# Row gathers for an attention ranking model: one tile moved to SyncE, single-SBUF-input VectorE operations, c inside the contraction, and a reordered last block

## The chip, the cores and the metric

The kernel runs on one core of a Trainium2 chip. The metric is device time in microseconds; the kernel before took 15,447.25 us (median of three runs, 15,437.24 to 15,494.0). Besides the timed runs there is one profiled execution, which took 11,178.86 us.

## The reference

For each of 16,384 users there are 69 item ids and one label id, all rows of a table `emb` of 100,001 rows with 96 floats. What is computed, cut to what matters:

```python
u = emb[batch_user]                       # 16384 x 69 x 96
ql = emb[batch_label[:, 0]]               # 16384 x 96
q = jnp.broadcast_to(ql[:, None, :], u.shape)
z = jnp.concatenate([q, u, q - u, q * u], axis=-1)
h = _dice(z @ W1 + b1, a1, EPS_DICE)      # 64 wide; dice(x) = (a*(1-p)+p)*x, p = sigmoid(x*s)
att = (h @ W2 + b2) @ W3 + b3             # one weight per item
pre = jnp.where((batch_user < ITEM_NUM)[..., None], u * att, 0.0)
pooled = jnp.einsum('gf,bfe->bge', window, pre)       # 69 items into 10 groups
x = jnp.concatenate([pooled.reshape(B, 10 * 96), ql], axis=-1)
h = _dice(_bn_eval(x @ Wf1 + bf1), af1)   # 200 wide
h = _dice(_bn_eval(h @ Wf2 + bf2), af2)   # 80 wide
return h @ Wf3 + bf3
```

An id of 100,000 counts as no item. The first layer is rewritten in both kernels as u (W1[1] - W1[2]) + (q*u) W1[3] + c, with c = q (W1[0] + W1[2]) + b1, one value per user and hidden unit.

## The kernel before

The users go in 32 blocks of 512. A block has 69 chunks of 512 (user, item) pairs, four tiles of 128 rows each: 64 main chunks (8 users by 64 items) and 5 tail chunks (one item of all 512 users). Two chunks make a pair; there are 1104 pairs, and the work of one pair is spread over several steps of a hand-made schedule.

Ids at or above 100,000 are mapped to an extra row of zeros (`rows`), by a VectorE operation with the ids as both inputs:

```python
nc.vector.scalar_tensor_tensor(rows, ids[:, 0:NT], float(ITEM_NUM), ids[:, 0:NT], ALU.is_ge, ALU.add)   # L110
```

GpSimd gathers each tile of 128 rows (L229); TensorE turns it; VectorE multiplies by q and ScalarE copies out of PSUM:

```python
def fetch(i):
    ...
    for t in range(4):
        gather(u[:, 4 * j + t, :], rows[n][:, 4 * k + t : 4 * k + t + 1])                   # L229
        nc.tensor.transpose(ptr[:, t * P : (t + 1) * P], u[:, 4 * j + t, :], ident)         # L325
    ... nc.vector.tensor_tensor(quT[:, j, :] ..., ptr ..., by_field(q ...), ALU.mult)       # L328
    nc.scalar.copy(uT[:, j, :], ptr)                                                        # L336
```

The label rows of blocks 1 to 31 are fetched by SyncE, one transfer per row, after 32 ids have been loaded from HBM into its registers:

```python
def head_gather(n, part):
    ...
    _, at = nc.values_load_multi_w_load_instructions(lab[n : n + 1, part * NLD : (part + 1) * NLD], ...)   # L252
    for i, row in enumerate(at):
        nc.sync.dma_start(out=qs[n][p + i : p + i + 1, k, :], in_=emb[bass.ds(row, 1), :])                 # L260
```

c is put into the accumulator before the matmuls: a matmul of zeros opens the bank, ScalarE writes c over it, and the first layer adds to it:

```python
def seed(i):
    nc.tensor.matmul(ph, zrow[:, 0:P], zrow, start=True, stop=False)                       # L295
    nc.scalar.copy(ph.rearrange(...), by_field(cs[n0][0][:, k0 * NS : (k0 + 1) * NS]))     # L298
def hidden(i, ph, uT, quT):
    for w, x, last in [(A, uT, False), (Wp, quT, True)]:
        for j in range(2):
            nc.tensor.matmul(ph[j * H1 : (j + 1) * H1, :], w, x[:, j, :], start=False, stop=last)   # L343
    nc.scalar.activation(y, ph, AF.Sigmoid, scale=S_DICE)                                  # L345
    nc.scalar.activation(y, y, AF.Identity, bias=a1c, scale=na1c)                          # L346
    nc.vector.tensor_mul(y, ph, y)                                                         # L347
```

Four pairs' attention weights are turned together and spread over the groups, then used as the moving side of the pooling:

```python
    nc.vector.tensor_scalar(w, pt[:, :, :, 0:2] ..., bb, None, ALU.add)                    # L373
    nc.vector.tensor_tensor(rw ..., R ..., w ..., ALU.mult)                                # L376, both in SBUF
    nc.tensor.matmul(pa[...], u[:, 4 * j + t, :], rw[:, i % 4, j, t, :], ...)              # L393
    nc.vector.tensor_copy(pooled[n][...], pa ...)                                          # L402
```

The three last layers of a block (L423, L437, L446) run in ten steps beside the next block; each dice ends in a product of two SBUF tiles (`nc.vector.tensor_mul(x1, x1, g1)`, L430, and L441). The result of a block goes out by SyncE (L449). [The set-up, with some twenty small loads, is left out here.]

Of the kernel before, what the change touches and what calls it, by code (L numbers as in the profile page):

```python
# [30 lines left out]
BF16 = mybir.dt.bfloat16  # L32
# [5 lines left out]
P = 128  # L38
# [16 lines left out]
NLD = 32  # L55
# [6 lines left out]


@with_exitstack
def rec_kernel(
# [3 lines left out]
    lab: bass.AP,  # L69
    emb: bass.AP,  # L70
    W1: bass.AP,
    b1: bass.AP,
    a1: bass.AP,
    W2T: bass.AP,
    b2: bass.AP,
    W3: bass.AP,
    b3: bass.AP,
    Wf1: bass.AP,
    bf1: bass.AP,
    af1: bass.AP,  # L80
    Wf2: bass.AP,
    bf2: bass.AP,
    af2: bass.AP,
    Wf3: bass.AP,
    bf3: bass.AP,
    wrow: bass.AP,
    wtile: bass.AP,
# [7 lines left out]
    tpool = ctx.enter_context(tc.tile_pool(name="tpool", bufs=5))  # L95
    hpool = ctx.enter_context(tc.tile_pool(name="hpool", bufs=3))
    ypool = ctx.enter_context(tc.tile_pool(name="ypool", bufs=8))
# [3 lines left out]

    def load_ids(n):
        ids = ipool.tile([P, NCOL], I32, tag="ids", name=f"ids{n}")
        nc.sync.dma_start(out=ids, in_=idx[n : n + 1].rearrange("o p n -> (o p) n"))
        return ids

    def map_ids(n, ids):

        rows = ipool.tile([P, NT], I32, tag="rows", name=f"rows{n}")
        nc.vector.scalar_tensor_tensor(rows, ids[:, 0:NT], float(ITEM_NUM), ids[:, 0:NT], ALU.is_ge, ALU.add)  # L110
        return rows

    ids, rows = {0: load_ids(0)}, {}
    rows[0] = map_ids(0, ids[0])
# [5 lines left out]
    w1 = const.tile([E, 4, H1], F32, name="w1")  # L120
    nc.sync.dma_start(out=w1, in_=W1.rearrange("(k e) h -> e k h", e=E))
    Cq = const.tile([E + 1, 2, H1], F32, name="Cq")
    for i in range(2):
        nc.vector.tensor_add(Cq[0:E, i, :], w1[:, 0, :], w1[:, 2, :])
    nc.sync.dma_start(
        out=Cq[E : E + 1], in_=b1.rearrange("(o q h) -> o q h", o=1, q=1).to_broadcast([1, 2, H1])
    )
    Wp = w1[:, 3, :]
    A = const.tile([E, H1], F32, name="A")
    nc.vector.tensor_sub(A, w1[:, 1, :], w1[:, 2, :])  # L130

    qTs = []
    for i in range(2):
        t = const.tile([E + 1, BLK + NS], F32, name=f"qT{i}")
        nc.vector.memset(t[:, BLK:], 0.0)
        nc.vector.memset(t[E : E + 1, :], 1.0)
        qTs.append(t)

    def column(ap, name, n, copies=1):
        t = const.tile([n * copies, 1], F32, name=name)  # L140
        for i in range(copies):
            nc.sync.dma_start(out=t[i * n : (i + 1) * n, :], in_=ap.rearrange("(n o) -> n o", o=1))
        return t

    def one_minus(t, name):
        r = const.tile(list(t.shape), F32, name=name)
        nc.vector.tensor_scalar(r, t, -1.0, 1.0, ALU.mult, ALU.add)
        return r

    a1c = column(a1, "a1c", H1, 2)  # L150
    na1c = one_minus(a1c, "na1c")


    w2t = const.tile([H2, 2, H1], F32, name="w2t")
    for i in range(2):
        nc.sync.dma_start(out=w2t[:, i, :], in_=W2T)
    w3 = const.tile([H2, 1], F32, name="w3")
    nc.sync.dma_start(out=w3, in_=W3)
    w3b = const.tile([H2, E], F32, name="w3b")
    nc.vector.tensor_copy(w3b, w3.to_broadcast([H2, E]))  # L160
    b2c = column(b2, "b2c", H2)
    b2m = const.tile([H2, P], F32, name="b2m")
    nc.vector.tensor_copy(b2m, b2c.to_broadcast([H2, P]))
    b3r = const.tile([P, 1], F32, name="b3r")
    nc.sync.dma_start(out=b3r, in_=b3.rearrange("(o n) -> o n", o=1).to_broadcast([P, 1]))
# [6 lines left out]
    R = const.tile([P, 2 * G], F32, name="R")  # L172
    nc.scalar.dma_start(out=R, in_=wtile)
    wr = const.tile([E, NTAIL, G], F32, name="wr")
    nc.scalar.dma_start(out=wr, in_=wrow.rearrange("(o f) g -> o f g", o=1).to_broadcast([E, NTAIL, G]))


    wf1 = const.tile([E, G + 1, D1], F32, name="wf1")
    nc.scalar.dma_start(out=wf1, in_=Wf1.rearrange("(k e) n -> e k n", e=E))
    wf2 = const.tile([DH, 2, D2], F32, name="wf2")  # L180
    nc.scalar.dma_start(out=wf2, in_=Wf2.rearrange("(k e) n -> e k n", e=DH))
    wf3 = const.tile([D2, 1], F32, name="wf3")
    nc.scalar.dma_start(out=wf3, in_=Wf3)
    bf1c = [column(bf1[i * DH : (i + 1) * DH], f"bf1c{i}", DH) for i in range(2)]
    af1c = [column(af1[i * DH : (i + 1) * DH], f"af1c{i}", DH) for i in range(2)]
    bf2c = column(bf2, "bf2c", D2)
    af2c = column(af2, "af2c", D2)
    bf3c = column(bf3, "bf3c", 1)
    naf1c = [one_minus(t, f"naf1c{i}") for i, t in enumerate(af1c)]
    naf2c = one_minus(af2c, "naf2c")  # L190
    sbf1 = []
    for i in range(2):
        t = const.tile([DH, 1], F32, name=f"sbf1_{i}")
        nc.vector.tensor_scalar_mul(t, bf1c[i], S_BN)
        sbf1.append(t)
    sbf2 = const.tile([D2, 1], F32, name="sbf2")
    nc.vector.tensor_scalar_mul(sbf2, bf2c, S_BN)

    zrow = const.tile([1, 512], BF16, name="zrow")
    nc.vector.memset(zrow, 0.0)  # L200

    with tc.tile_pool(name="prep_ps", bufs=1, space=PSUM) as pps:
        pv = pps.tile([P, E], F32, name="pv")
        nc.tensor.matmul(pv, w2t.rearrange("a i h -> a (i h)"), w3b, start=True, stop=True)
        nc.vector.tensor_copy(vrep, pv)
        for i in range(2):
            nc.vector.tensor_copy(v2[i * H1 : (i + 1) * H1, i : i + 1], pv[i * H1 : (i + 1) * H1, 0:1])
        pb = pps.tile([P, 1], F32, name="pb")
        nc.tensor.matmul(pb, b2m, w3, start=True, stop=True)
        nc.vector.tensor_add(bb, pb, b3r)  # L210
# [17 lines left out]
    def gather(dst, index):  # L228
        nc.gpsimd.indirect_dma_start(  # L229
            out=dst,  # L230
            out_offset=None,
            in_=emb,
            in_offset=bass.IndirectOffsetOnAxis(ap=index, axis=0),
        )

    def chunk(c):

        return divmod(c, NCH)

    def first_head():  # L240

        q = bpool.tile([P, NQ, E], F32, tag="q", name="q0")
        for k in range(NQ):
            gather(q[:, k, :], ids[0][:, NT + k : NT + k + 1])
        return q

    def head_gather(n, part):

        if part == 0:
            qs[n] = bpool.tile([P, NQ, E], F32, tag="q", name=f"q{n}")  # L250
        k, p = divmod(part * NLD, P)
        _, at = nc.values_load_multi_w_load_instructions(  # L252
            lab[n : n + 1, part * NLD : (part + 1) * NLD],
            engines=[mybir.EngineType.SP],
            min_val=0,
            max_val=ITEM_NUM,
            skip_runtime_bounds_check_because="labels are rows of the table",
        )
        for i, row in enumerate(at):
            nc.sync.dma_start(out=qs[n][p + i : p + i + 1, k, :], in_=emb[bass.ds(row, 1), :])  # L260
# [7 lines left out]
    def head_row(n):  # L268

        cT = bpool.tile([P, BLK], F32, tag="cT", name=f"cT{n}")  # L270
        pc = ps_x.tile([P, BLK], F32, tag="x", name=f"pc{n}")
        for i in range(2):
            nc.tensor.matmul(
                pc[i * H1 : (i + 1) * H1, :],
                Cq[:, i, :],
                qTs[n % 2][:, i * NS : i * NS + BLK],
                start=True,
                stop=True,
            )
        nc.scalar.copy(cT, pc)  # L280

        cU = bpool.tile([P, BLK], F32, tag="cU", name=f"cU{n}")
        pc = ps_x.tile([P, BLK], F32, tag="x", name=f"pc2_{n}")
        nc.tensor.matmul(pc, Cq.rearrange("e i h -> e (i h)"), qTs[n % 2][:, 0:BLK], start=True, stop=True)
        nc.scalar.copy(cU, pc)
        return cT, cU

    def by_field(ap):

        return ap.rearrange("e (s o) -> e s o", o=1).to_broadcast([ap.shape[0], NS, FM])  # L290

    def seed(i):

        ph = ps_h.tile([P, 512], F32, tag="h", name=f"ph{i}")
        nc.tensor.matmul(ph, zrow[:, 0:P], zrow, start=True, stop=False)  # L295
        (n0, k0), (n1, k1) = chunk(2 * i), chunk(2 * i + 1)
        if n0 == n1 and k1 < NMAIN:
            nc.scalar.copy(  # L298
                ph.rearrange("h (s f) -> h s f", f=FM), by_field(cs[n0][0][:, k0 * NS : (k0 + 1) * NS])
            )  # L300
        elif n0 == n1 and k0 >= NMAIN:
            nc.scalar.copy(ph, cs[n0][1])
        else:
            for j, (n, k) in enumerate([(n0, k0), (n1, k1)]):
                lo, hi = j * H1, (j + 1) * H1
                if k < NMAIN:
                    nc.scalar.copy(
                        ph[lo:hi].rearrange("h (s f) -> h s f", f=FM),
                        by_field(cs[n][1][lo:hi, k * NS : (k + 1) * NS]),
# [264 lines left out]
```

## Time and profile before

| | us |
|---|---|
| timed, median of three | 15,447.25 |
| profiled execution, span | 11,177.1 |
| GpSimd busy / idle before gathers | 8404.8 / 2692.9 |
| TensorE busy | 9700.5 |
| ScalarE busy | 3760.0 |
| VectorE busy | 3187.3 |
| mean granted TensorE clock | 0.707 |

The clock changes between 0.5 and 1.0 of full speed all through the span. A matmul of float32 shows as two records in the groups. [...] The times of the profile are those of one execution, and they are a good deal shorter than the timed ones.

### The profile page before, as it was taken

The numbers are of one execution on the slowest core, as the hardware profiler recorded it, in microseconds if no ns is written. First come the engines' busy times: TensorE is split into PE (matmuls) and PEld (weight loads), VectorE is DVE, ScalarE is ACT, GpSimd is POOL, SyncE is SP. The second block draws the span as 40 slices with busy tenths as digits, with TensorE's granted clock in tenths as the row PEclk, the third lists the DMA queues.
The fourth block names the chain that finished last, engine by engine and source line by source line (L and its number), as shares of the span: only waits on it lengthen the run. The fifth ranks groups of instructions, "written<-read, shape, count | busy, mean of one in ns | idle before, by whom it ended". The sixth has DMA issues, their size and how long they took to land.

```text
span 11177.1 us, 157529 instructions
## 1 busy us (share of the span) xinstructions
PE 9700.5 (87%) x41348; PEld 4721.0 (42%) x41348; DVE 3187.3 (29%) x5424; ACT 3760.0 (34%) x6086; POOL 8404.8 (75%) x8842
## 2 busy tenths in 40 slices
PE   6888888888888898888888888888888888988888
PEld 3444444444444444444444444444444344444444
DVE  2222222222222222222222222222222222222222
ACT  2333333333333333333333333333333333333332
POOL 7777777777777777777777777777777777777775
PEclk6767677677776767767777667776677776677767
DMA  2222222222222222222222222222222222222221
GB/s 45 41 41 41 41 41 41 41 41 41 41 41 41 41 41 41 41 42 41 41 41 41 41 41 41 40 41 42 41 41 41 41 42 41 41 41 41 41 40 29
DMA packets 323169, 456.81 MB, mean 41 GB/s; under 512 B 175712, under 2 KB 180864, under 8 KB 322272
## 3 DMA queue, kind: packets, MB, share of 16 engines
q0 software_dynamic: 282752, 434.87, 19.6%
q1 hardware_dynamic: 37886, 10.92, 0.5%
q8 instruction: 333, 5.46, 0.2%
q14 instruction: 564, 4.62, 0.1%
q10 hardware_dynamic: 1634, 0.94, 0.0%
HBM read 446.04 MB, written 0.07 MB: 40 GB/s over the span
## 4 chain that ended last, share of the span: by engine, by line
PE 33%; POOL 32%; issue 16%; DMA 10%; SPq 5%; ACT 2%; DVE 1%; POOLq 0%; ACTq 0%
POOL u L229 32%; PE ph L343 12%; DMA u<-in_emb,rows 10%; PE acc L393 9%; PE p L423 4%; SPq L260 3%; PE ptr L325 3%; PE prow L354 2%; SPq L252 2%; PE ph L295 2%; PE pa L363 1%; ACT y L346 1%; DVE y L347 1%; ACT y L345 1%; PE patt L370 1%
## 5 line engine op out<-in xcount | busy, mean ns | idle before, releaser
L229 POOL DMA_INDIRECT u<-in_emb,rows x8832 | 8400.1, 951 | 2692.9 <-issue 2459.0
L325 PE MATMUL ptr<-ident,u 128*96 128x128 f32 x8832 | 2006.4, 353 | 1189.5 <-DMA u<-in_emb,rows 1172.1
L325 PEld LDWEIGHTS ptr<-ident,u 128*96 128x96 f32 x8832 | 1221.0, 155 | 3053.7 <-DMA u<-in_emb,rows 1526.9
L393 PEld LDWEIGHTS acc<-rw,u 128*96 128x96 f32 x16384 | 2048.5, 217 | 531.8 <-issue 531.2
L393 PE MATMUL acc<-rw,u 128*96 128x20 f32 x16384 | 2160.4, 282 | 1.8 <-DVE rw L376 1.3
L336 ACT COPY uT<-ptr 96x512 f32<-96x512 f32 x2208 | 1283.4, 581 | 2207.0 <-DVE quT L328 2039.4
L347 DVE TENSOR_TENSOR y<-ph,y 128x512 f32<-128x512 f32 x1104 | 763.5, 692 | 4394.8 <-ACT y L346 4292.3
L345 ACT ACTIVATE y<-ph 128x512 f32<-128x512 f32 x1104 | 659.1, 597 | 3754.1 <-PE ph L343 3753.9
L343 PE MATMUL ph<-uT,A 96*64 96x512 f32 x4416 | 1793.5, 904 | 0.0
L343 PE MATMUL ph<-quT,w 96*64 96x512 f32 x4416 | 1671.9, 847 | 0.0
L328 DVE TENSOR_TENSOR quT<-ptr,qT 96x512 f32<-96x512 f32 x2048 | 1348.9, 679 | 611.5 <-PE ptr L325 607.0
L402 DVE COPY pooled<-acc 96x160 f32<-96x160 f32 x1008 | 433.3, 430 | 2189.9 <-PE acc L393 2184.4
L346 ACT ACTIVATE y<-y,a1c,na1c 128x512 f32<-128x512 f32 x1104 | 897.2, 813 | 36.6
L343 PEld LDWEIGHTS ph<-quT,w 96*64 96x64 f32 x4416 | 442.8, 194 | 1074.9 <-issue 1074.9
L298 ACT COPY ph<-cT 128x512 f32<-128x512 f32 x1008 | 591.3, 587 | 498.2 <-PE ph L295 497.8
L295 PE MATMUL ph<-zrow 1*128 1x512 bf16 x1104 | 527.6, 478 | 193.4 <-DVE y L347 191.7
L423 PE MATMUL p<-pooled,wf 96*100 96x512 f32 x1280 | 659.4, 660 | 1.2 <-DVE x L427 0.8
L343 PEld LDWEIGHTS ph<-uT,A 96*64 96x64 f32 x4416 | 282.6, 177 | 550.0 <-issue 464.8
L354 PE MATMUL prow<-y,v 128*32 128x512 f32 x2208 | 455.2, 909 | 0.0
L356 ACT COPY row<-prow 128x512 f32<-128x512 f32 x276 | 161.5, 585 | 628.4 <-PE prow L354 622.9
L423 PEld LDWEIGHTS p<-pooled,wf 96*100 96x100 f32 x1280 | 232.2, 190 | 287.7 <-issue 285.5
L423 PE MATMUL p<-pre,V 96*100 96x512 f32 x640 | 314.6, 625 | 0.0
(71 smaller groups left out, 2318.5 us busy)
## 6 DMA issues: line engine op xcount, KB each, us to landing
q<-in_emb SPq DMA_DIRECT2D x15872, 0.4 KB
u<-in_emb,rows POOLq DMA_INDIRECT x8832
ids<-in_idx SPq DMA_DIRECT2D x32, 140.0 KB
wf<-in_Wf ACTq DMA_DIRECT2D x1, 825.0 KB
out<-res SPq DMA_DIRECT2D x32, 2.0 KB
w<-in_W SPq DMA_DIRECT2D x1, 96.0 KB
q<-in_emb,ids POOLq DMA_INDIRECT x4
wf<-in_Wf ACTq DMA_DIRECT2D x1, 62.5 KB
```

Source lines behind the costliest of these rows:

```text
L229: nc.gpsimd.indirect_dma_start(out=dst, out_offset=None, in_=emb, in_offset=bass.IndirectOffsetOnAxis(ap=index, axis=0),)
L295: nc.tensor.matmul(ph, zrow[:, 0:P], zrow, start=True, stop=False)
L325: nc.tensor.transpose(ptr[:, t * P : (t + 1) * P], u[:, 4 * j + t, :], ident)
L328: nc.vector.tensor_tensor(quT[:, j, :].rearrange("e (s f) -> e s f", f=FM), ptr.rearrange("e (s f) -> e s f", f=FM), by_field(q[:, k * NS ...
L336: nc.scalar.copy(uT[:, j, :], ptr)
L343: nc.tensor.matmul(ph[j * H1 : (j + 1) * H1, :], w, x[:, j, :], start=False, stop=last)
L345: nc.scalar.activation(y, ph, AF.Sigmoid, scale=S_DICE)
L346: nc.scalar.activation(y, y, AF.Identity, bias=a1c, scale=na1c)
L347: nc.vector.tensor_mul(y, ph, y)
L354: nc.tensor.matmul(pr[32 * k : 32 * (k + 1), :], v2, y, start=True, stop=True)
L393: nc.tensor.matmul(pa[:, j, 2 * t : 2 * t + 2, :].rearrange("e n g -> e (n g)"), u[:, 4 * j + t, :], rw[:, i % 4, j, t, :], start=True, st ...
L423: nc.tensor.matmul(p1, w[:, h * DH : (h + 1) * DH], x, start=(k == 0), stop=(k == KTOP - 1))
```

## The change

- **Ids.** A second table `rows`, with zeros in row 100,000, takes the place of the mapping; the labels keep `emb`. The ids of the SyncE rows are loaded into SBUF once per block and into the registers from there.
- **SyncE.** Besides the 512 label rows, it fetches the 128 rows of one tile per block (of blocks 1 to 31), which GpSimd then need not gather.
- **VectorE.** Operations with two inputs in SBUF are replaced by such as take one from PSUM, because VectorE's second SBUF input can hold up GpSimd.
- **c.** The 32 free contraction rows (96 to 127) hold a 0/1 pattern beside u and c of 32 users beside the weights, so the matmul adds c by itself. Tail chunks get one more matmul instead. The seed is gone.
- **Last block.** Its tail chunks come first, its last eight pairs have a plan of their own, and its last layers run in quarters of 128 users. Results stay in SBUF, and go out in two stores at the end.
- **Set-up.** The weights come in two packed loads.

The core of the diff (cuts marked):

```diff
-        _, at = nc.values_load_multi_w_load_instructions(
-            lab[n : n + 1, part * NLD : (part + 1) * NLD],
+    def load_solo(n):
+        t = spool.tile([(NQ + 1) * PARTS, NLD], I32, tag="sid", name=f"sid{n}")
+        nc.sync.dma_start(out=t, in_=solo[n])
+        return t
+    def fetch_rows(table, dst, index):
+        _, at = nc.values_load_multi_w_load_instructions(index, ...)
+        for i, row in enumerate(at):
+            nc.sync.dma_start(out=dst[i : i + 1, :], in_=table[bass.ds(row, 1), :])
 ...
-                gather(u[:, 4 * j + t, :], rows[n][:, 4 * k + t : 4 * k + t + 1])
-                nc.tensor.transpose(ptr[:, t * P : (t + 1) * P], u[:, 4 * j + t, :], ident)
+                if n > 0 and 4 * k + t == SOLO:
+                    tiles.append(solos.pop(n))
+                else:
+                    tiles.append(u[:, 4 * j + t, :])
+                    gather(rows, tiles[-1], ids[n][:, 4 * k + t : 4 * k + t + 1])
+                nc.tensor.transpose(ptr[:, t * P : (t + 1) * P], tiles[-1], ident)
 ...
-    def hidden(i, ph, uT, quT):
-        for w, x, last in [(A, uT, False), (Wp, quT, True)]:
-            for j in range(2):
-                nc.tensor.matmul(ph[j * H1 : (j + 1) * H1, :], w, x[:, j, :], start=False, stop=last)
+        for (n, k), p in zip(places, sums):
+            if k >= NMAIN:
+                nc.tensor.matmul(p, Cq, qTs[n % 2], start=True, stop=False)
+        for j, ((n, k), p) in enumerate(zip(places, sums)):
+            if k < NMAIN:
+                nc.tensor.matmul(p, As[n % 2][:, k // 4, :], uT[j], start=True, stop=False)
+            else:
+                nc.tensor.matmul(p, A, uT[j][0:E], start=False, stop=False)
+        for j, p in enumerate(sums):
+            nc.tensor.matmul(p, Wp, quT[:, j, :], start=False, stop=True)
 ...
-        nc.vector.tensor_scalar(w, pt[:, :, :, 0:2].rearrange("p t k j -> p k j t"), bb, None, ALU.add)
-        nc.vector.tensor_tensor(rw ..., R ..., w ..., ALU.mult)
+        for j in range(2):
+            nc.vector.scalar_tensor_tensor(rw[:, :, j, :], pt ... , bb, R ..., ALU.add, ALU.mult)
 ...
-        nc.vector.tensor_scalar(x1, p1, S_BN, sbf1[h], ALU.mult, ALU.add)
-        nc.scalar.activation(g1, x1, AF.Sigmoid, scale=S_DICE)
-        nc.scalar.activation(g1, g1, AF.Identity, bias=af1c[h], scale=naf1c[h])
-        nc.vector.tensor_mul(x1, x1, g1)
+        nc.scalar.activation(g, p, AF.Sigmoid, bias=sb, scale=S_BN * S_DICE)
+        nc.scalar.activation(g, g, AF.Identity, bias=sa, scale=sna)
+        nc.vector.scalar_tensor_tensor(x, p, b, g, ALU.add, ALU.mult)
 ...
     def chunk(c):
-        return divmod(c, NCH)
+        n, k = divmod(c, NCH)
+        if n == NBLK - 1:
+            k = (k - NTAIL) % NCH
+        return n, k
 ... [the plan of the last eight pairs, the quarters, the stores and the packed weights are cut]
```

## The prediction

> **What bounds the kernel now.** I read the busy times first, then the costliest groups, then the waits.
>
> ```profile
> PE 9700.5 (87%) x41348; PEld 4721.0 (42%) x41348; DVE 3187.3 (29%) x5424; ACT 3760.0 (34%) x6086; POOL 8404.8 (75%) x8842
> L229 POOL DMA_INDIRECT u<-in_emb,rows x8832 | 8400.1, 951 | 2692.9 <-issue 2459.0
> L325 PE MATMUL ptr<-ident,u 128*96 128x128 f32 x8832 | 2006.4, 353 | 1189.5 <-DMA u<-in_emb,rows 1172.1
> ```
>
> TensorE looks busiest (87%), but the second line decides. GpSimd issues 8832 table gathers (plus 4 for the first labels), one 951 ns each, and its 2692.9 us of idle time is nearly all "issue": time in which it waited for nothing. That is 305 ns after every gather. Busy plus idle, 8400.1 + 2692.9 = 11,093 us, is the whole span of 11,177 us but for 84. The third line is the counterproof: TensorE waits 1172 us for gathered rows to land, and hardly anything in the other direction. The engine that is "75% busy" is the full one. The records of its gathers say the same: the start-to-start time is 1.248 us at the 25th, 50th and 90th percentile, the first starts at 3.4 us, the last ends at 11,101 us, and there is no gap above 3 us.
>
> So the span is 3.4 us of start, 8836 gathers at 1.2485 us plus what lengthens some of them (11,098 us together), and 76 us after the last.
>
> Two gathers are longer than the usual 0.94 us, from the order of time of two stretches:
>
> ```profile
> 5061.18 0.69 DVE L430 TENSOR_TENSOR x<-x,g 100x512 f32<-100x512 f32 x1 [1.54 <-ACT g L429]
> 5061.29 1.40 POOL L229 DMA_INDIRECT u<-in_emb,rows  x1 [0.30 <-issue]
> ...
> 5188.80 0.83 DVE L376 TENSOR_TENSOR rw<-R,w 128x640 f32<-128x640 f32 x1
> 5189.06 1.38 POOL L229 DMA_INDIRECT u<-in_emb,rows  x1 [0.30 <-issue]
> ```
>
> Both began while VectorE ran an operation with two inputs in SBUF. The tail, in order of time:
>
> ```profile
> 11100.36 0.94 POOL L229 DMA_INDIRECT u<-in_emb,rows  x1 [0.30 <-issue]
> ...
> 11132.79 12.10 PE L423 MATMUL p<-pooled,wf 96*100 96x512 f32 x20 [0.38 <-DVE pooled L408]
> ...
> 11174.89 0.22 SPq L449 DMA_DIRECT2D out<-res  x1
> ```
>
> 32 us of pooling, then 42 us of the last block's three layers, with nothing beside them.
>
> **The gap between profile and time.** The profiled execution took 11,178.9 us, the timed ones 15,437 to 15,494. Nothing in the trace accounts for the missing 4268 us. The granted clock cannot do it alone: in stretches of 35 us and more at clock 0.5, TensorE still made one pair of chunks (eight tiles) per 9.6 us, while 15,447 us over 1104 pairs is 14.0. I treat the gap as unknown: either a constant beside the span, or the same work at a slower rate (15,447 / 11,177 = 1.382).
>
> **What the Trainium skill says.** "SBUF — State Buffer", section "Who interferes with whom": a VectorE instruction with two SBUF inputs contends with a GpSimd instruction that reads SBUF; with at most one SBUF input, outside the two-port modes, it does not. In a bracket it infers that descriptor generation needs only the write side, so that tensor_tensor should leave gathers alone. The trace agrees with the first and not with the bracket: gathers overlapped by, or just after, the L376 multiply run 122 ns over the usual on average, those near L430 286 ns, those near L328 (one input in PSUM) 2 ns.
> "DMA: Bandwidth & Descriptors", section "SWDGE vs HWDGE vs iDMA": transfers issued from SyncE never touch GpSimd's descriptor rings. That is the point of moving a tile to SyncE; the 15,872 row transfers there already leave the gathers' spacing alone.
> "Perfetto Trace Analysis", section "DMA Instruction — SWDGE (GPSIMD)": a gather's bar is descriptor generation, not data movement. The trace agrees: the queue of the gathers fills 19.6% of the DMA engines' time, so fewer bytes per gather would buy nothing; fewer gathers would.
>
> **The change, part by part.**
> One tile per block to SyncE: blocks 1 to 31 lose one gather of 276 each, 31 x 1.2485 = 39 us, on the path.
> No two-SBUF operations: summing each gather's excess over 943 ns gives 78 us in all. L376 (276 times 0.83 us), L430 and L441 (96), L110 (32) lie beside nearly all of it and all go: the new forms take one input straight from PSUM. I count 68 us; about 10 remain with the start's tail weights (L224) and chance.
> c by 32 more contraction rows: the seed matmul (L295, 528 us busy), its ScalarE copy (L298, 591 us) and the wait for it disappear for 1104 pairs. In their place 160 tail chunks get one matmul of 97 rows by 512; a pair of chunks takes 1.0 to 2.0 us in L343, so 80 to 160 us. TensorE sheds 350 to 450 of 9700 us. A matmul of 128 rows should last as long as one of 96. All this lies beside the gathers: worth 0 to the span.
> Constants in two loads instead of some twenty: the first gather waits for the ids alone (3.4 us). 0.
> Results kept in SBUF, one store: SyncE loses 2230 us of waiting for results. Off the path.
> Last block: tail chunks first, three of four quarters of the layers ahead of or between the last pools. After the last gather remain two hidden layers, four pools (1.5 to 2.7 us each), two quarters of 32 matmuls over 128 columns (L423 shows 0.45 us per 512-column record at full clock, two records a matmul, so 0.23 us a matmul, twice that at half clock: 15 to 28 us), and two dice chains. I take 40 us for 76: 36 saved.
> Sum: 39 + 68 + 36 = 143 us; the span becomes about 11,035 us (8805 gathers x 1.2485 = 10,993, + 10, + 3, + about 30 to 40 after them).
> For the time: 15,447 - 143 = 15,304 if the gap is a constant; 15,447 x 11,035 / 11,177 = 15,251 if all is slower in proportion. I say 15,280, or 1.1% less.
>
> **Does SyncE keep up?** This is the first rival.
>
> ```profile
> 5209.58 156.53 SPq L260 DMA_DIRECT2D q<-in_emb  x288
> SPq L449 <- DVE res L448: 2230.6, 31, 350.3
> PE pq L265 <- DMA q<-in_emb: 50.3, 24, 46.4
> ```
>
> 288 rows in 156.5 us are 0.544 us a row, 278 us for the 512 of a block, of the 349 a block lasts. Within a group of 32 the rows follow at 0.403 us; the rest, 4.9 us a group, is the load of 32 ids from HBM (1.2 + 3.6 us). The change makes 640 rows: 258 us and 20 loads. If a load from SBUF costs the same, 356 us per block, more than the 344 (275 x 1.2485 = 343) that the gathers take: SyncE would become the bound, 31 x 356 plus the start and end, some 11,200 us, and the gain is gone (about 15,480). At half the cost 307 us, and it is hidden. The third line shows it was nearly late once before (46 us, block 1), without a hole in the gathers. I hold hidden for likelier: the ids move next to the engine for this very purpose, and waiting for results goes too.
>
> **Other rivals.** TensorE is what is really full in the timed runs, at a clock the profile does not show. Then the 4 to 5% of work shed counts: some 14,750. For it: 87% busy, and clock 0.5 in 59% of the span. Against it: the 9.6 us per pair above.
> The gap grows with the data handed over. The table is given twice now (38.4 MB more beside some 44 MB). If 4268 us were the handing over of 44 MB, it would add 3.7 ms: 19,000. Against it: times are device times, and the kernel reads no more bytes than before.
> Contention is much dearer in timed runs: at most 404 removed VectorE operations of 0.4 to 0.83 us, 315 us in all, if each held up GpSimd for its whole length; with the rest, 15,050.
>
> **Range and chances.** The main line (GpSimd bound, gains of 1%) spreads from 15,200 to 15,350; SyncE as bound reaches 15,480; TensorE as bound 14,750. I take 14,900 to 15,430. Faster by over 2% needs 15,138 or less: TensorE or dear contention, 0.23. Slower by over 2%: the second table, or an order of work that stalls, 0.13. Within 2%: 0.64.
>
> **What would show each step.** Right: 8805 gathers, mean near 944 ns and "issue" still ending their idle time; no gather above 1.1 us in the middle; under 50 us after the last; no seed copies; SyncE's groups of 32 at 13 to 16 us. Wrong: gathers waiting for TensorE or for a buffer, a wait of the transpose for SyncE's tile, gathers still stretched, or a span near 11,030 whose time moved by something else than 1%: then the gap holds the answer.

## The result, and the profile after

The changed kernel takes **16,758.99 us** (median of four runs, 16,737.84 to 16,797.88) against 15,444.53 for the kernel before (four runs): a ratio of 1.0847, interval 1.0816 to 1.0877. It is 8.5% slower; the prediction was 1.1% faster.

This time the profiled execution took as long as the timed ones (16,737.84 us), so its trace shows what they wait for. From the page, the busy times and three of the costliest groups (busy and mean ns of one, then idle before them and what ended most of it):

```profile
PE 8968.4 (54%) x41797; PEld 4652.8 (28%) x41797; DVE 2996.2 (18%) x5324; ACT 3157.6 (19%) x4969; POOL 8330.0 (50%) x8811
L256 POOL DMA_INDIRECT u<-in_rows,ids x8801 | 8325.3, 946 | 8276.4 <-PE acc L428 3973.5
L308 PE MATMUL pq<-ident,q 128*96 128x128 f32 x128 | 42.8, 368 | 3800.4 <-DMA q<-in_emb 3796.0
L344 PE MATMUL ptr<-ident,u 128*96 128x128 f32 x8801 | 1458.0, 308 | 705.8 <-issue 429.2
```

The gathers are as predicted, in number and in length (946 ns). But GpSimd's idle time is now 8276 us, and its largest part ends with a matmul, not with "issue". The third line says why: TensorE waits 3796 us for `q`, the label rows that SyncE fetches. The view of waits (total us, times, longest) has it too; its third line below shows one long wait per block:

```profile
POOL u L256 <- PE acc L428: 3973.5, 120, 127.0
PE pq L308 <- DMA q<-in_emb: 3796.0, 63, 73.6
DVE qT L309 <- PE pq L308: 3618.2, 31, 127.2
```

31 times, 117 us on average, the block can't begin: its last label rows have not come. TensorE stands meanwhile (0.42 us busy in the first stretch of 105 us below); the gathered tiles are not used up, GpSimd gets no free buffer and stands too. SyncE is the engine that sets the pace. Its own work in order of time (start, us, rows on the right), around one such stop:

```profile
5100.61 46.46 SPq L293 DMA_DIRECT2D q<-in_emb  x97
...
5150.12 55.09 SPq L293 DMA_DIRECT2D q<-in_emb  x116
...
5212.56 129.57 SPq L293 DMA_DIRECT2D solo<-in_rows  x128
...
5345.84 313.87 SPq L293 DMA_DIRECT2D q<-in_emb  x384
```

The first two lines are 0.48 us a row, loads of ids included: as expected. The last two are 1.01 and 0.82 us a row. What differs is whether the other engines work. The busy time of the engines in two stretches (PE, PEld, DVE, ACT, POOL, then clock, DMA share, GB/s):

```profile
5100.00:5205.00 105.00, 0.42 (x1) 0.16 (x1) 0.00 (x0) 0.00 (x0) 0.00 (x0) 0.50 0.01 3
5215.00:5345.00 130.00, 75.69 (x382) 42.73 (x380) 25.66 (x46) 27.77 (x44) 84.80 (x90) 0.67 0.18 35
```

SyncE is slow while GpSimd gathers and the others work, and quick while all of them stand; which of them it is, the experiments have to tell. It isn't only the instruction that starts a transfer that lengthens. For the label rows, SyncE's records of one instruction (shortest, median and longest ns):

```profile
L293 SPq MOVE q<-in_emb x15872: 1/29/1398, 9.6 to 16137.2; - x199
L293 SPq DMA_DIRECT2D q<-in_emb x15872: 1/225/1407, 9.7 to 16137.3; - x199
```

The same in the kernel before's trace, on which the prediction rests:

```profile
L260 SPq MOVE q<-in_emb x15872: 29/29/38, 16.9 to 10571.0; - x199
L260 SPq DMA_DIRECT2D q<-in_emb x15872: 219/220/343, 16.9 to 10571.1; - x199
```

A MOVE is one of the register instructions that go with each row. It takes 29 ns, never over 38 there; here up to 1398. Of the 2506 MOVEs over 60 ns in this trace, half took 0.69 to 0.71 us, and 27 about twice that. TensorE's matmuls come late as well. In the changed kernel, in order of time (idle time before it in brackets):

```profile
5075.52 0.62 PE L384 MATMUL prow<-y,v 128*32 128x512 f32 x1
5076.69 0.59 PE L384 MATMUL prow<-y,v 128*32 128x512 f32 x1 [0.56 <-issue]
5078.11 1.01 PE L384 MATMUL prow<-y,v 128*32 128x512 f32 x1 [0.82 <-issue]
5079.51 1.76 PE L384 MATMUL prow<-y,v 128*32 128x512 f32 x2 [0.39 <-issue]
```

From the second on they start 1.42 and 1.40 us apart, again twice 0.70. In the kernel before's trace all eight matmuls of such a group take 1.06 us:

```profile
5020.70 1.06 PE L354 MATMUL prow<-y,v 128*32 128x512 f32 x8
```

So the two traces differ in more than the change. Something holds up the instruction streams of SyncE and TensorE in one of them. Below, an execution with such steps is called **held**, one without them **free**; both kinds occurred with the same kernel, as the experiments show.

### The profile page after: what moved, and what is told of

Its sections match the earlier page's. It is cut to its first block, busy times and chain, and to the rows that moved or that the text cites. A ratio compares the mean times of both kernels' runs of the same rounds, so it can differ in the third digit from the quotient of the medians.

```text
span 16736.1 us, 169286 instructions
## 1 busy us (share of the span) xinstructions
PE 8968.4 (54%) x41797; PEld 4652.8 (28%) x41797; DVE 2996.2 (18%) x5324; ACT 3157.6 (19%) x4969; POOL 8330.0 (50%) x8811
## 5 line engine op out<-in xcount | busy, mean ns | idle before, releaser
L256 POOL DMA_INDIRECT u<-in_rows,ids x8801 | 8325.3, 946 | 8276.4 <-PE acc L428 3973.5
L344 PE MATMUL ptr<-ident,u 128*96 128x128 f32 x8801 | 1458.0, 308 | 705.8 <-issue 429.2
L373 PE MATMUL ph<-quT,wn 96*64 96x512 f32 x4416 | 1671.4, 770 | 121.1 <-issue 118.7
L369 PE MATMUL ph<-uT,A 128*64 128x512 f32 x4096 | 1683.1, 846 | 73.6 <-issue 71.1
L384 PE MATMUL prow<-y,v 128*32 128x512 f32 x2208 | 750.0, 890 | 377.6 <-issue 238.7
L376 ACT ACTIVATE y<-y,wn,na1c 128x512 f32<-128x512 f32 x1104 | 897.4, 813 | 37.1
L373 PEld LDWEIGHTS ph<-quT,wn 96*64 96x64 f32 x4416 | 451.2, 180 | 1184.9 <-issue 1184.3
L467 PE MATMUL p<-pooled,wf 96*100 96x512 f32 (+1 forms) x1400 | 644.3, 591 | 45.8 <-issue 40.9
L369 PEld LDWEIGHTS ph<-uT,A 128*64 128x64 f32 x4096 | 283.6, 170 | 637.9 <-issue 618.5
L401 PE MATMUL patt<-ident,row 128*128 128x128 f32 x1108 | 243.6, 342 | 280.1 <-issue 162.3
```

Source lines behind the costliest of these rows:

```text
L256: nc.gpsimd.indirect_dma_start(out=dst, out_offset=None, in_=table, in_offset=bass.IndirectOffsetOnAxis(ap=index, axis=0),)
L344: nc.tensor.transpose(ptr[:, t * P : (t + 1) * P], tiles[-1], ident)
L369: nc.tensor.matmul(p, As[n % 2][:, k // 4, :], uT[j], start=True, stop=False)
L373: nc.tensor.matmul(p, Wp, quT[:, j, :], start=False, stop=True)
L384: nc.tensor.matmul(pr[32 * k : 32 * (k + 1), :], v2, ys[b + k], start=True, stop=True)
L467: nc.tensor.matmul(p1, w[:, h * DH : (h + 1) * DH], x, start=(k == 0), stop=(k == KTOP - 1))
```

## The experiments

They ran in five groups, each with the kernel before timed beside it. That kernel took 11,185 us in the first group and 11,194 in the fourth (free), and 15,482, 15,756 and 15,719 in the second, third and fifth (held). Times are compared within a group; between groups, ratios are. The theories named by letters in the expectations: A, SyncE's rows bound the changed kernel; B and C, another part of the change does it (the new first layer, order of work, or the second table). A2 is A with SyncE alone held up; E says that TensorE is held up as well.

### First group (free)

**The kernel before, unchanged**, to see it profiled once more.

> The kernel before, unchanged, to get the trace of an execution as slow as the timed ones. Theory A (SyncE's row transfers bound both kernels; while gathers run, SyncE needs about twice as long per row as the first profile showed): about 15,440 us, the transposes of the label rows wait for SyncE for thousands of us, gathers have holes. Rival B (the change of the first layer and of the order of work is what costs): about 15,440 us, and no wait for SyncE's rows worth mentioning. If the span is near 11,180 again, both are without the state they have to explain.

Measured: 11,185.33 us. That settles what the prediction left "unknown": the 4268 us between profile and times are no constant beside the span. There are executions of the whole kernel in 11,185 us. The held condition itself was missed here.

**No tile on SyncE**: all other parts of the change, with GpSimd gathering the tile.

```diff
-                if n > 0 and 4 * k + t == SOLO:
+                if False:
-            for part in range((NQ + 1) * PARTS):
+            for part in range(NQ * PARTS):
```

> The changed kernel, but GpSimd gathers the tile that SyncE took over; SyncE keeps the 512 label rows per block. Theory A: the time follows the rows, 640 to 512, so 16,760 x 0.8 = 13,400 us (13,000 to 13,900), under the kernel before as well, since the ids come from SBUF. Rival B (first layer, order of work): 16,700 us or a little more. Rival C (a second table costs): 16,700.

Measured: 11,104.58 us, ratio 0.9927 (0.9911 to 0.9944). Every number expected was for held executions, so all missed. It still rules out much: with the new first layer, order, set-up and second table, the kernel gains 0.7%. Together they cost nothing in a free execution. Its rows, and two waits of its view of waits:

```profile
L293 SPq MOVE q<-in_emb x15872: 29/29/29, 9.5 to 10415.5; - x199
L293 SPq DMA_DIRECT2D q<-in_emb x15872: 224/225/305, 9.5 to 10415.5; - x199
```

```profile
POOL u L256 <- issue: 2501.7, 8205, 0.3
...
PE ptr L344 <- DMA u<-in_rows,ids: 2035.2, 2422, 2.4
```

MOVEs of 29 ns without exception, GpSimd waiting for nothing, TensorE waiting for gathers: the picture that the prediction drew.

**All by GpSimd**: as above, and the label rows gathered too; SyncE fetches no rows.

```diff
-            gather(emb, q[:, k, :], ids[0][:, NT + k : NT + k + 1])
+            gather(emb, q[:, k, :], ids[n][:, NT + k : NT + k + 1])
 ...
-            for part in range((NQ + 1) * PARTS):
-                at(first - 32 + part, lambda n=n, part=part: solo_part(n, part))
+            at(first - 17, lambda n=n: qs.__setitem__(n, head_q(n)))
```

> The changed kernel, but with no row transfers on SyncE at all: GpSimd gathers the four label tiles of a block too, 8960 gathers. Theory A: GpSimd becomes the bound, 8960 x 1.2485 + 50 = 11,240 us (11,150 to 11,400), and profile and timed runs agree. Rivals B and C: well above 15,000, because they blame what is still in this kernel.

Measured: 11,255.96 us, 1.0063 (1.0046 to 1.008), as expected: 124 more gathers than without the tile, 151 us.

**The kernel before with its ids in SBUF**.

```diff
+            nc.sync.dma_start(out=sids[n], in_=lab[n : n + 1, :].rearrange("o (a b) -> (o a) b", b=NLD))
 ...
-            lab[n : n + 1, part * NLD : (part + 1) * NLD],
+            sids[n][part : part + 1, :],
```

> The kernel before, with one part of the change alone: the label ids are loaded into SBUF once per block, and into SyncE's registers from there. Theory A: 16 loads per block get shorter by about 2.5 us each, so 31 x 16 x 2.5 = 1200 us less, 14,200 us (13,700 to 14,700). Rivals B and C: unchanged, 15,440.

Measured: 11,185.9 us, 1.0000 (0.9991 to 1.0009). Where SyncE is hidden, a cheaper load of ids is worth nothing. The expectation was for held executions.

### Second group (held)

**The changed kernel, unchanged.**

> The changed kernel, unchanged, where the kernel before takes 11,185 us and SyncE's rows follow at 0.40 us. Theory A (SyncE's rows bound the timed runs of the result, because its instructions were stretched there; nothing else of the change costs): 640 x 0.408 + 20 x 2.1 = 303 us per block on SyncE, hidden beside 344 us of gathers; 8805 x 1.2485 + 70 = 11,065 us (11,040 to 11,090), 1.1% less than before. Rival B (order of work, first layer): well above 11,185. If SyncE's instructions are stretched again: 16,760 for this one, 15,440 for before.

Measured: 16,767.29 us, 1.0818 (1.0795 to 1.084), with MOVEs up to 1401 ns again. Counting rows per stretch of 5 us over the whole trace, stretches with a load of ids left out: where GpSimd starts no gather SyncE makes 11.3, where it gathers without pause (four or more starts) 4.7 if TensorE works too, 2.6 if TensorE stands. In the kernel before's free trace, with gathers without pause, it makes 10.8. So SyncE is slow beside gathers even where TensorE does nothing.

**Every row transfer twice**, the second into a tile that nobody reads; first in the kernel before, then in the changed one.

```diff
             nc.sync.dma_start(out=qs[n][p + i : p + i + 1, k, :], in_=emb[bass.ds(row, 1), :])
+            nc.sync.dma_start(out=twins[0][p + i : p + i + 1, :], in_=emb[bass.ds(row, 1), :])
```

> The kernel before, with each of SyncE's row transfers issued twice, the second into a tile that nobody reads: SyncE's cost per row doubled, nothing else touched. Theory A (SyncE's cost per row is what made 11,185 into 15,444): 512 x 0.81 + 16 x 4.9 = 491 us per block, 31 x 491 plus start and end = 15,300 to 15,900. Rival D (the timed runs were slow for another reason, e.g. slower gathers or a slower clock): the doubled rows stay mostly hidden, under 12,500.

> The changed kernel with each of SyncE's row transfers issued twice. Theory A: 640 x 0.81 + 20 x 2.1 = 561 us per block, 17,400 to 17,900, and a ratio to the doubled kernel before of 1.10 to 1.15, that is the sign and the size of the measured 1.085. Rival D: no slower than the doubled kernel before.

Measured: 22,390.36 us (1.4448, 1.439 to 1.4506) and 25,200.34 us (1.6261, 1.6218 to 1.6305). Both times expected assumed a free SyncE and are far off; the ratio of the two, 1.1255, is as expected. The doubled kernel before adds 6908 us for 15,872 rows: 0.435 us a row, somewhat more than the 0.403 that one takes on SyncE. A SyncE with time to spare would have swallowed a part. So **SyncE bounds the kernel before as well**, in a held execution. The changed one adds 8433 us for 19,840 rows, 0.425 each. Both wait where the changed kernel waits; the doubled kernel before:

```profile
PE pq L269 <- DMA q<-in_emb: 6807.7, 61, 124.3
```

The doubled changed kernel:

```profile
PE pq L313 <- DMA q<-in_emb: 11297.8, 123, 116.5
```

**Two tiles on SyncE, labels by GpSimd**: 256 rows a block on SyncE in place of 640.

```diff
-SOLO = 4 * 8
+SOLOS = [32, 64]
```

> A version made to bear a slow SyncE: GpSimd gathers the label tiles, SyncE two main tiles of a block (256 rows). 8898 gathers x 1.2485 + 65 = 11,175 us (11,150 to 11,200) where SyncE is quick; where its rows take a microsecond, 256 + 17 us per block stay hidden and the time is the same.

Measured: 16,732.7 us, 1.0798 (1.0776 to 1.0821), by a defect of this version: the load of the next block's ids stood on SyncE's queue behind row transfers that waited for the single buffer, and GpSimd's gathers waited for the ids:

```profile
POOL q L257 <- DMA ids<-in_idx: 3775.6, 32, 128.4
```

It says nothing of the theory, and was mended in the next group.

### Third group (held)

**All by GpSimd, again** (the edit of above).

> The kernel of e3 (no row transfers on SyncE), now hoped for on a chip where the kernel before takes 15,440 us. Theory A2 (there, SyncE makes no headway for about 0.8 us of every gather, so a block costs SyncE its own time plus 205 to 235 us: before 286 + 205, after 304 + 228, doubled 492 + 219 and 565 + 235): with no rows, GpSimd bounds, 8960 gathers, 11,250 us (11,150 to 11,450). Rival E (there, TensorE is held up as well, and enough to bound): over 12,500.

Measured: 13,281.21 us, 0.8428 (0.8391 to 0.8466). The version without the tile, next below, still has 512 rows a block and takes 15,234 us: without them 1953 us are gone. But 2025 us over the 11,256 of this version in a free execution stay. The chain that ended last, and a group:

```profile
PE 53%; issue 21%; another core or an unknown queue 14%; POOL 6%; DVE 3%; ACT 2%; DMA 1%; DVEq 0%; POOLq 0%
...
L347 PE MATMUL ptr<-ident,u 128*96 128x128 f32 x8832 | 1638.5, 320 | 1679.3 <-issue 1301.9
```

TensorE's idle time ahead of the turning of tiles is now ended by "issue", not by gathered data: its own instructions come late. The view of waits shows the same on VectorE:

```profile
DVE y L380 <- issue: 648.7, 124, 23.2
```

In all, 877 us of VectorE's idle time and 931 of ScalarE's end in "issue" here, where the view of this version's free trace lists none. A2 falls; E is right that TensorE is held up as well, and VectorE and ScalarE are late too. Which of the three costs the 2025 us was not tried; the chain lies on TensorE for 53%, and on waits whose releaser the profile doesn't name ("another core or an unknown queue") for 14%.

**No tile, again.**

> The kernel of e2 (512 rows on SyncE, ids from SBUF, first layer and order of the change). Where before takes 15,440: theory A2 says 512 x 0.408 + 16 x 2.1 + 220 = 463 us per block, 31 x 463 + 250 = 14,600 (14,200 to 15,000), less than before; rival E says 15,400 or more. Where before takes 11,185: 11,104 as in e2.

Measured: 15,234.38 us, 0.9666 (0.9621 to 0.9711): less gain than A2 expected (14,600), but a gain. Its wait at the beginning of a block:

```profile
DVE qT L309 <- PE pq L308: 1948.0, 31, 118.9
```

SyncE bounds it still, 62.8 us of waiting a block where the changed kernel has 116.7. The 54 us between are close to what 128 rows and four loads of ids take on a free SyncE (61 us).

**No gathers**: the changed kernel with every gather of main and tail tiles replaced by a fill. This leaves out the look-up of those tiles.

```diff
-                    gather(rows, tiles[-1], ids[n][:, 4 * k + t : 4 * k + t + 1])
+                    nc.gpsimd.memset(tiles[-1], 0.0)
```

> The changed kernel with each gather of a tile replaced by a GpSimd fill with zeros (leaves the table reads of the main and tail tiles out; SyncE's 640 rows per block stay). Theory A2: with no gathers SyncE is never held up, also where before takes 15,440: rows at 0.41 us, no stretched instructions, and the span is TensorE's or SyncE's own, 9,500 to 10,800 us. If SyncE's instructions are stretched here too, the gathers are not the cause.

Measured: 10,021.63 us (one execution), in a group in which the kernel before took 15,756 and all other executions were held. The rows, and the chain:

```profile
L293 SPq MOVE q<-in_emb x15872: 3/29/29, 9.4 to 9649.9; - x199
L293 SPq DMA_DIRECT2D q<-in_emb x15872: 2/225/540, 9.5 to 9650.0; - x199
```

```profile
SPq 64%; issue 23%; PE 12%; ACT 1%; DMA 0%; DVE 0%
```

No MOVE over 29 ns. **It is the gathers that hold SyncE up**, and neither its number of rows nor the work of TensorE, which goes on. The chain shows besides that SyncE, free, is the bound of this version: 10,022 us over 31 blocks is 323 us a block, of which its rows and loads take 304.

**Two tiles on SyncE, mended**: ids through ScalarE's queue, two buffers for the tiles.

> e8 mended: its ids load sat on SyncE's queue behind row transfers that waited for a buffer; now the ids come by ScalarE's queue and the tiles have two buffers. GpSimd gathers the labels, SyncE two tiles per block. Theory A2, where before takes 15,440: 256 x 0.408 + 8 x 2.1 + 220 = 341 us per block, just hidden: 11,175 to 11,600. Where before takes 11,185: 8898 x 1.2485 + 65 = 11,175.

Measured: 14,069.86 us, 0.8927 (0.8886 to 0.8967). Fewer rows than the kernel before, and faster; more than none, and slower than none. It is far above the 11,175 to 11,600 expected, which had GpSimd as the bound and left TensorE's late instructions out; without any rows the time was 13,281 already. A wait of GpSimd that the trace without rows doesn't have is large enough for the 789 us between the two: before a block's label gathers it stands 26 us, until rows of SyncE have landed.

```profile
POOL q L257 <- DMA solo<-in_rows: 811.6, 31, 30.8
```

### Fourth group (free)

**The tile alone, on the kernel before**, with its ids still loaded from HBM.

```diff
+                if n > 0 and 4 * k + t == SOLO:
+                    tiles.append(solos.pop(n))
-            for part in range(BLK // NLD):
+            for part in range((BLK + P) // NLD):
```

> The kernel before with one part of the change alone: SyncE also fetches one main tile per block (640 rows instead of 512, ids from HBM as before). Theory A3 (where before takes 15,440 to 15,760: gathers hold up the instruction streams of SyncE and TensorE; SyncE is the bound, and the tile's 384 instructions per block are what made the change slower): 356 us of its own + 214 = 570 per block, 17,900 us (17,200 to 18,300), 1.10 to 1.16 times before. Rival B (order of work, first layer): within 1% of before. Where before takes 11,185: 356 us per block is over the gathers' 344: 11,250 to 11,500.

Measured: 11,570.81 us, 1.034 (1.0321 to 1.0358), 71 us above the range for a free execution. Two of its waits:

```profile
POOL u L233 <- issue: 2475.5, 8093, 8.2
PE pq L271 <- DMA q<-in_emb: 2004.0, 47, 71.9
```

The second line is SyncE as bound even when it is free: 11,571 over 31 is 373 us a block. 640 rows and 20 loads from HBM make 356, by the prediction's own figures. The tile needs the ids in SBUF merely to fit.

**Ids in SBUF, kernel before, again.**

> The kernel of e4 (before, ids from SBUF). Where before takes 15,440 to 15,760: theory A3 gives 16 shorter loads per block, 2.5 us each, but e10 showed less than that for this and all other parts but the tile together, so 0.96 to 0.99 times before. Rival (the loads don't matter, the other parts gave e10 its gain): 1.00.

Measured: 11,189.2 us, 1.0003 (0.9985 to 1.0021). Free again; its effect in held executions was not seen.

**Plain transfers in place of gathers**: GpSimd moves 128 neighbouring rows per tile; then the same issued by ScalarE. Both leave out the look-up.

```diff
-                    gather(rows, tiles[-1], ids[n][:, 4 * k + t : 4 * k + t + 1])
+                    at = (4 * (2 * i + j) + t) % 700 * P
+                    nc.gpsimd.dma_start(out=tiles[-1], in_=rows[at : at + P, :])
```

> The changed kernel, each table gather replaced by a plain transfer of 128 neighbouring rows of the table, still issued by GpSimd (leaves the look-up by id out, keeps GpSimd's making of descriptors and the traffic). If the making of descriptors or the traffic holds SyncE up: rows stretched as before where before takes 15,440, 14,000 to 17,000 us. If it is the reading of the ids from SBUF: rows at 0.41 us, 10,000 to 11,500 us.

> As e15, but issued by ScalarE's queue, so that GpSimd makes no descriptors and the traffic stays. If GpSimd's making of descriptors holds SyncE up: rows at 0.41 us, no stretched instructions, 10,000 to 11,500 us also where before takes 15,440. If the traffic does: stretched, over 13,000.

Measured: 10,032.44 and 18,276.18 us (one execution each). The group was free, so the first tells nothing yet. The second doesn't answer its question at all: with ScalarE as the issuer the data come late, and TensorE waits for them. Its queue in the table of queues (packets, MB, share), and that wait:

```profile
q10 hardware_dynamic: 1267488, 434.39, 10.7%
```

```profile
PE ptr L345 <- DMA u<-in_rows: 6149.2, 3699, 3.5
```

### Fifth group (held)

**The changed kernel once more**, and **plain transfers by GpSimd** beside it.

> The changed kernel, unchanged. Theory A3 where before takes 11,185 us: SyncE's 303 us per block stay hidden, 8805 gathers x 1.2485 + 70 = 11,065 (11,040 to 11,090), 0.989 times before, and 40 less than e2. Where before takes 15,440: 16,760 as before. Rival B (order of work or first layer cost something everywhere): over 11,185 in either case.

> e15 again (plain transfers of neighbouring rows by GpSimd in place of the gathers). Where before takes 15,440: if GpSimd's making of descriptors or the traffic stretches SyncE's instructions, 12,000 us or more and rows far over 0.41 us; if it is the gather by ids, 10,030. Where before takes 11,185: 10,030 as in e15.

Measured: 17,050.3 us, 1.0836 (1.0808 to 1.0863), the ratio that A3 expected, with a MOVE up to 1424 ns; and 10,035.72 us (one execution) for the plain transfers. The rows of the latter, then its group of transfers from the page:

```profile
L293 SPq MOVE q<-in_emb x15872: 3/29/397, 9.5 to 9661.5; - x199
L293 SPq DMA_DIRECT2D q<-in_emb x15872: 3/225/304, 9.6 to 9661.6; - x199
```

```profile
L344 POOL DMA_DIRECT2D u<-in_rows x8801 | 4633.1, 539 | 5268.5 <-PE acc L429 4966.4 <-issue 275.5 <-PE ptr L345 17.8
```

Only one MOVE is over 60 ns. GpSimd's queue in the table of queues, in the result's trace of the changed kernel and here:

```profile
q0 software_dynamic: 281760, 433.35, 13.0%
...
q0 software_dynamic: 281760, 433.35, 17.5%
```

In a group where gathers hold SyncE up, 8801 plain transfers of the same bytes in the same number of packets don't. So it is neither the bytes on the way nor that GpSimd issues the transfers. It is something in the indirect form: its reading of ids, its scattered rows, or what else GpSimd does in its 0.94 us. These three were not told apart.

## Why the prediction was wrong

**The step that failed** is "Does SyncE keep up?". It took a row as 0.403 us and 156.5 us for 288 of them from a trace of a free execution, and used them for runs that were held. There SyncE was the bound before the change: a block took 498 us (15,445 / 31), not 349. It had no room for 128 more rows. The step held "hidden" for likelier because of the 307 us at half the load cost, and that sum was nearly right: on a free SyncE, a load from SBUF shows 2.13 us in the trace, so 640 x 0.408 + 20 x 2.13 = 304. What it lacked is the time that gathers take from SyncE.

How large that is can be worked out, as an estimate: a block's measured time less what SyncE's rows and loads take when free.

| held execution | block (time / 31), us | SyncE's own, us | difference, us |
|---|---|---|---|
| before | 498 | 286 | 212 |
| before, rows doubled | 722 | 493 | 229 |
| changed, no tile | 491 | 243 | 248 |
| changed | 541 | 304 | 237 |
| changed, rows doubled | 813 | 565 | 248 |

The difference stays between 212 and 248 us while SyncE's work more than doubles, and without gathers it is 19 us (323 less 304). There are 275 or 276 gathers a block in each line: some 0.8 to 0.9 us of SyncE's time per gather. So one more row costs its own full time, and one gather less brings back only those 0.8 to 0.9 us. The tile: (1.0836 - 0.9666) x 15,719 = 1839 us by measurement (two groups), 31 x (128 x 0.408 + 4 x 2.13) = 1883 us by working. All other parts together: (0.9666 - 1) x 15,719 = -525 us. The two add up to the +1314 us of the fifth group by construction; the result's 16,759 - 15,445 is 1314 as well.

**"The gap between profile and time"** is where this lay. The prediction set 4268 us aside as "a constant beside the span, or the same work at a slower rate". It was neither: another engine was the bound. The step should have asked which streams, slowed, could make 15,445.

**SyncE as the bound**, the first rival, was the right kind. Its size, 15,480, fell short by 1280 us: it had SyncE overtake the gathers by 12 us a block (356 for 344), where in held executions all 59 us of the tile's rows and loads (1839 / 31) come on top.

**39 us for 31 gathers less**: right in count (8805 with the first labels); in held executions not on the path.

**68 us for two-SBUF operations**: the mechanism held. Summed over 943 ns, the gathers' excess is 13 us in the free version without the tile and 26 in the changed kernel, for 78 before: 52 to 65 us gained, on the path in free executions alone. Without two-SBUF operations the lengthened gathers are nearly gone. Against the bracket in the Trainium skill, "SBUF — State Buffer", section "Who interferes with whom", the prediction goes too far: the bracket infers only that descriptor generation is left alone, and these gathers also take their ids from SBUF, so the section's own rule on GpSimd instructions that read SBUF covers them. No run here puts such operations beside plain transfers.

**36 us of tail**: mis-sized. In the free version without the tile the last gather ends at 11,040.3 of 11,104.4 us: 64 us remain, not 40; 12 saved. The first gather starts at 6.9 us, not 3.4.

**Shed work of TensorE** (350 to 450 us): more than that, 9700 to 8958 in the free version without the tile. A first-layer matmul over 128 rows took 870 ns there, one over 96 rows 904 before: about as long, as assumed. What the shed work is worth was not tried alone.

**Rivals.** "TensorE is what is really full": in part. With SyncE's rows away the chain lies mostly on it at 13,281 us, at a mean clock of 0.728, no lower than the 0.707 of the profile before: its instructions come late. The second table: the version without the tile has it too, and takes 11,105 us free and 0.9666 of the kernel before held. Dear contention: in the held trace of the doubled kernel before, the gathers' excess sums to 61 us, no more than the 78 of the free one.

**What stays open.** The changed kernel was met in held executions only. That it would gain about 1% free (11,105 less some 39) is argued, not measured. What makes a session held or free is not known: two chips showed both. And the parts without the tile bring 525 us, 17 a block, while the cheaper loads alone relieve SyncE by 43 a block (286 less 243). Where the other 26 go was not tried. How an indirect gather holds up other engines, and why only in some executions, no run shows.

## What to carry to other kernels

When the profile and the times of the same kernel differ by 38%, the profile's bound is not the bound of the times; ask which instruction stream would make up the difference, and move no work onto it. In held executions, row transfers issued one by one at 0.4 us are not free beside indirect gathers: taking 19,840 of them away, for 155 more gathers, saved (1.0836 - 0.8428) x 15,719 = 3785 us here. The best version met there has no rows on SyncE at all (13,281 us, 0.8428 of the kernel before), and it loses only 0.6% in free ones.

## What the hardware showed unexpectedly

- Indirect gathers on GpSimd can hold up SyncE's instructions, most often by 0.70 us (a MOVE of 29 ns takes up to 1.4 us), while the gathers themselves keep their 0.94 us. In the same executions instructions of TensorE, VectorE and ScalarE come late too (with no rows on SyncE, 1314, 649 and 555 us of idle time end in "issue" in their largest groups). The same kernel took 11,185 or some 15,500 us. "DMA: Bandwidth & Descriptors", section "SWDGE vs HWDGE vs iDMA", in the Trainium skill has transfers issued from SyncE stay clear of GpSimd's descriptor rings; here they are slowed all the same, in the instructions that issue them.
- Fills (0.18 us each) and plain transfers (0.54 us each) on GpSimd did nothing of the kind to SyncE, in one execution each among held ones.
- Tile loads of 128 rows by 96 floats issued by ScalarE's queue made 1,267,488 packets, and the kernel 18,276 us; by GpSimd's queue it took 10,032.
